# Pinning the scaling of a scan's rows in ScalarE's program order, two slots ahead of the step

## The chip, the cores and the metric

The kernel runs on one core of a Trainium2 chip. The metric is the device time of one execution in microseconds; the time of a kernel is the median of several runs. Engines are named as in the profile: PE is TensorE (PEld its weight loads), ACT is ScalarE, DVE is VectorE, POOL is GpSimd, SP issues DMAs.

## The reference

For `x` of 32 sequences of 256 tokens with 256 channels, the result is `x + ffn(cond(x))`. The first block, `cond`, is a gated state-space layer; the second has two layers of local attention and a gated feed-forward. What matters here is the scan in `cond`:

```python
xr, gate = jnp.split(x @ W_in.T, 2, axis=-1)
xr = xr + t_emb[:, None, :]
...
xn = (xc - mu) / jnp.sqrt(var + 1e-05) * ln_g + ln_b
Bm, Cm, dt = jnp.split(xn @ W_xproj.T, 3, axis=-1)
...
def step(h, inputs):
    ad, bd, xt, ct = inputs
    h = jnp.clip(h * ad[:, :, None] + bd[:, :, None] * xt[:, None, :], -10.0, 10.0)
    yt = jnp.einsum('bd,bdh->bh', ct, h)
    return (h, yt)
```

Every token is one step; the state of a sequence is 16 x 512 numbers. The second block has, for each sequence and layer, projections to q, k and v, softmax over a window of 128, and `a * gelu(g)` between two projections.

## The kernel before

**The scan.** The 32 sequences are worked in four groups of eight. With 16 states and 8 sequences the state `h` of a group fills 128 partitions x 512. A group has 256 steps, cut into 8 chunks of 32 tokens. The decay is divided out beforehand (a running product `pd`), so that a step (`step`, L665) is one VectorE instruction: add the scaled row to `h` and clip it to limits that belong to the token. Its input is a row: `xn` of token t, repeated over the 16 states and multiplied by `beta`, one number for each partition.

Each row goes through three places in the program. `load_rows` (L637), on SP's queue, loads 256 KB from `xnd` in device memory, repeated over the partitions, into a buffer `xrep` of which there are seven. `scale_row` (L658), on ScalarE, multiplies it in place by `beta`. `step` reads it on VectorE and so frees the buffer for a later load. In the first group, whose scan has no other work beside it (`alone`), half of the rows are repeated by TensorE instead (`spread_rows`, tile `bx` in PSUM) and scaled from there into an `xrep` buffer. Every fourth step, four `h` tiles are read by TensorE into `y` (`read_out`, L677).

**Slots.** The work of a group is entered into agendas by slot: slot t of a group is the place of its step t, and everything else has an offset from that. A group has two agendas: within a slot all of the first part comes ahead of the second. Loads stand at t-6 and scalings at t-1, both in the second part. The first part also holds, on ScalarE, the tanh of the convolution (`conv_th`), the copy of the raw sums, the normalising (`norm_apply`, `xn`), the squares (`norm_out`, `sq_x`), the gates and the output copy. `beta` of a chunk is ready by five slots ahead of its first step (`decays`, L606).

**The interleaving.** Attention and feed-forward of a sequence and layer are cut into stages (eight for a sequence, several sequences in flight). After each stage about two slots of the next group's scan are written into the program, so the scan of groups 1 to 3 runs beside attention and feed-forward of the groups before; the last group's have no scan beside them. All PSUM tiles of both parts share one pool of eight banks: softmax (`pT`, L1127), copies (`qT`, `kT`, `v_sb`) and gelu (`ag`, L1255) on ScalarE, and the product `ag` (L1263) on VectorE must read a bank before TensorE can have it again.

**The order on an engine.** The order written down is not the order executed. A scheduler walks the program with modelled durations and gives each engine the earliest written instruction that it believes ready[...]. An instruction whose inputs the model has as landed can therefore stand ahead of ones written before it. `tc.keep_in_program_order(ins)` ties `ins` to the instruction written before it on the same engine: it may not be issued ahead of that one. It is an ordering for the scheduler and adds no semaphore. The kernel uses it in a few places on GpSimd.

Of the kernel before, what the change touches and what calls it, by code (L numbers as in the profile page):

```python
# [73 lines left out]
def kernel(  # L74
# [29 lines left out]
    nc = tc.nc  # L104
# [111 lines left out]
    for i in range(2):  # L216
        t = const.tile([P, NI * (P + GB)], FP, tag=f"ly{i}", name=f"ly{i}")
# [3 lines left out]
    def program(ctx, exact):  # L221
# [163 lines left out]
        def group_scan(g):  # L385
# [8 lines left out]
            alone = g == 0  # L394
# [5 lines left out]
            def at(s, what, *args):  # L400
                agendas[-1].setdefault(s, []).append(partial(what, *args))
# [229 lines left out]
            def by_tensor(t):  # L631
                return alone and t % NQ < XR
# [21 lines left out]
            def scale_row(c, t):  # L654
                if by_tensor(t):
                    ck[c]["rep", t] = xp.tile([P, DI], FP, tag="xrep", name="xrep")
                bx = ck[c]["rep", t]
                nc.scalar.activation(  # L658
                    bx, ck[c].pop(("bx", t), bx), AF.Copy, scale=ck[c]["beta"][:, t : t + 1]
                )  # L660

            def step(c, t):
                bx = ck[c].pop(("rep", t))
                h_new = hp.tile([P, DI], FP, tag="h", name="h")
                nc.vector._custom_dve(  # L665
                    TENSOR_ADD_SAT, out=h_new, in0=state["h"], in1=bx,
                    s0=ck[c]["lim"][:, 0, t : t + 1], s1=ck[c]["lim"][:, 1, t : t + 1],
                )
                ck[c]["h", t] = state["h"] = h_new
# [131 lines left out]
            for c in range(NCH):  # L801
                s0 = c * CH
# [35 lines left out]
            for c in range(NCH):  # L838
                s0 = c * CH
                at(s0 - 43, load_x, c)  # L840
                for ch in range(NC_):
                    at(s0 - 40 + 2 * ch, project, c, ch)
                for ch, s in enumerate((13, 16, 17, 18)):
                    at(s0 + s, project, c, NC_ + ch)
                at(s0 - 27, raw_sums, c)
                for j in range(NJ):
                    at(s0 - 26 + 4 * j, norm_turn, c, j)
                at(s0 - 8, figures_out, c)
                for t in range(CH):
                    if not by_tensor(t):  # L850
                        at(s0 + t - 6, load_rows, c, t)
                    if by_tensor(t) and t % XR == 0:
                        at(s0 + t - 4, spread_rows, c, t)
                    at(s0 + t - 1, scale_row, c, t)
                for hb in range(CH // TB):
                    s = s0 + hb * TB
                    at(s - 9 if alone else s + 7, load_skip, c, hb)
                    at(s + 23, out_turn, c)
                for d in range(KM):
                    at(s0 + 43 + 2 * d, project_y, c, d)  # L860
# [3 lines left out]
        def scan_slots(groups):  # L864


            slots, scans = {}, [group_scan(g) for g in groups]
            for part in range(2):
                for i, agendas in enumerate(scans):
                    for s, what in agendas[part].items():  # L870
                        slots.setdefault(i * S + s, []).extend(what)
            for s in range(min(slots), max(slots) + 1):
                for what in slots.get(s, ()):
                    what()
                yield s
# [525 lines left out]
        s0 = done[0]  # L1401
# [130 lines left out]
```

## Time and profile before

| | us |
|---|---|
| median of 3 runs | 3999.52 (3998.8 to 4003.98) |
| profiled execution | 3989.48 |
| its span, first to last instruction | 3987.7 |
| first and last scaling (L658) | 50.7 to 3104.3 |
| ScalarE busy | 2321.3 |
| VectorE busy | 2638.7 |
| loads of a row (L637) | 896, of 256 KB |

The span is what the profile's views refer to. A group's line gives the instruction's line, engine and tiles, then its total and mean duration, and then the idle time of its engine just before it with what ended it. A wait line says who waited for whom, with the total in us, how often, and the longest. What an idle engine costs depends on whether another engine waits for it.

### The profile page before, as it was taken

The page shows a single profiled execution, that of the slowest core. Times are in us where ns is not written, and L with a number is a line of the kernel's source. Part 1 is how long each engine was busy: PE and PEld are TensorE (multiplying, and loading weights), DVE is VectorE, ACT ScalarE, POOL GpSimd, SP SyncE. Part 2 cuts the span into 40 slices and gives each one's busy share as a digit, 9 for nine tenths or more (in the row PEclk, how much of TensorE's full clock was granted, in tenths as well). Part 3 has the DMA queues.
Part 4 walks back from the last instruction along what each step waited for, and adds up shares of the span by engine and source line. Part 5 has one row for each costly group of instructions (what it writes and reads, how often), then busy time and mean ns, then how long its engine had stood idle before and what let it go on. Part 6 is the DMA issues. An engine that isn't in the chain of part 4 may idle for free.

```text
span 3987.7 us, 57891 instructions
## 1 busy us (share of the span) xinstructions
PE 3769.4 (95%) x20540; PEld 2359.2 (59%) x20540; DVE 2638.7 (66%) x5241; ACT 2321.3 (58%) x3893; POOL 1739.2 (44%) x1784
## 2 busy tenths in 40 slices
PE   7899889999999999999999999999999999999999
PEld 3333345666656666666666666566666666666666
DVE  6888887777766766767676677676677544444443
ACT  3555556666666566566666656556666555555553
POOL 4443364444444444544445444344444343433431
PEclk8999899999999999999999999999999999999999
DMA  5444533333433434233343434323333111000000
GB/s 152 116 119 118 159 111 110 89 107 103 106 98 97 124 109 128 84 93 94 91 112 94 118 106 116 101 83 101 94 101 103 36 36 44 1 17 20 18 14 23
DMA packets 360414, 353.51 MB, mean 89 GB/s; under 512 B 173795, under 2 KB 220212, under 8 KB 359988
## 3 DMA queue, kind: packets, MB, share of 16 engines
q1 hardware_dynamic: 275666, 337.71, 29.4%
q10 hardware_dynamic: 84450, 12.01, 1.9%
q8 instruction: 165, 2.70, 0.3%
q14 instruction: 133, 1.09, 0.1%
HBM read 314.49 MB, written 33.55 MB: 87 GB/s over the span
## 4 chain that ended last, share of the span: by engine, by line
PE 44%; DVE 16%; ACT 13%; DMA 11%; POOL 9%; issue 5%; ACTq 1%; SPq 0%; DVEq 0%; POOLq 0%
DMA xrep<-xnd 10%; PE ps_qkv L912 9%; PE pa L1247 8%; PE po_f L1275 5%; DVE h L665 5%; PE y L677 3%; ACT xrep L658 3%; PE ps_wo L962 3%; PE sc L1118 3%; PE ov L1156 2%; POOL rn L944 2%; ACT L1255 2%; DVE acc L454 2%; PE ps_in L407 2%; ACT L1127 2%
## 5 line engine op out<-in xcount | busy, mean ns | idle before, releaser
L658 ACT ACTIVATE xrep<-xrep,beta 128x512 f32<-128x512 f32 x896 | 631.1, 722 | 692.2 <-DMA xrep<-xnd 532.4
L665 DVE CUSTOM_DVE_ANT_0 h<-h,xrep,lim 128x512 f32<-128x512 f32 x1024 | 918.6, 897 | 52.7 <-PE y L677 12.5
L912 PE MATMUL ps_qkv<-qkv,res 128*128 128x512 f32 x1536 | 718.0, 604 | 34.6 <-ACT qT L956 21.7
L1247 PE MATMUL pa<-hT,w 128*128 128x256 f32 (+1 forms) x3072 | 693.0, 388 | 28.0 <-ACT pT L1127 26.8
L936 POOL TENSOR_TENSOR rot<-rot,swp 128x512 f32<-128x512 f32 x256 | 344.1, 1344 | 766.3 <-DVE swp L933 621.5
L1247 PEld LDWEIGHTS pa<-hT,w 128*128 128x128 f32 (+1 forms) x3072 | 502.4, 179 | 192.1 <-issue 63.3
L1263 DVE SCALAR_TENSOR_TENSOR ag<-pa,b_sb,ag 128x256 f32<-128x256 f32 (+1 forms) x448 | 213.1, 476 | 594.6 <-ACT ag L1255 593.2
L912 PEld LDWEIGHTS ps_qkv<-qkv,res 128*128 128x128 f32 x1536 | 279.2, 192 | 314.6 <-issue 247.4
L944 POOL TENSOR_TENSOR rn<-ss,neg_half 128x8 f32<-128x8 f32 x256 | 444.2, 1735 | 11.5 <-DVE ss L942 1.6
L1275 PE MATMUL po_f<-ag,w 128*128 128x256 f32 (+1 forms) x1536 | 385.4, 392 | 17.9 <-DVE res L1286 9.3
L677 PE MATMUL y<-h,ly 128*32 128x512 f32 x2048 | 369.1, 620 | 20.1 <-DVE h L665 19.5
L1275 PEld LDWEIGHTS po_f<-ag,w 128*128 128x128 f32 (+1 forms) x1536 | 273.9, 189 | 124.3 <-issue 44.4
L407 PE MATMUL ps_in<-xg,w_in_sb 128*128 128x256 f32 x1024 | 285.9, 410 | 18.0 <-DMA xg<-in_xT_dram 10.4
L945 POOL TENSOR_TENSOR rot<-rot,rn 128x512 f32<-128x512 f32 x256 | 287.7, 1124 | 20.0
L1206 POOL TENSOR_TENSOR rstd<-ve,neg_half 128x1 f32<-128x1 f32 x128 | 77.0, 602 | 486.6 <-DVE ve L1204 486.6
L407 PEld LDWEIGHTS ps_in<-xg,w_in_sb 128*128 128x128 f32 x1024 | 190.8, 199 | 145.7 <-issue 62.0
L928 DVE TENSOR_TENSOR rot<-ps_qkv,rc_sb 128x512 f32<-128x512 f32 x256 | 175.6, 686 | 139.0 <-ACT sq L925 137.8
L1127 ACT ACTIVATE pT<-sc 128x512 f32<-128x512 f32 x384 | 208.3, 594 | 94.9 <-PE sc L1118 93.3
L454 DVE SCALAR_TENSOR_TENSOR acc<-xr,wc_sb,acc 128x256 f32<-128x256 f32 x384 | 203.4, 532 | 89.2 <-POOL acc L443 88.1
L1127 ACT ACT_TABLE_LOAD x185 | 237.4, 1283 | 24.5 <-PE sc L1118 21.5
L1255 ACT ACTIVATE ag<-pa,b_sb 128x256 f32<-128x256 f32 x320 | 151.7, 474 | 156.8 <-PE pa L1247 152.4
L1255 ACT ACT_TABLE_LOAD x186 | 238.6, 1283 | 3.3
(149 smaller groups left out, 5765.7 us busy)
## 6 DMA issues: line engine op xcount, KB each, us to landing
xrep<-xnd SPq DMA_DIRECT2D x896, 256.0 KB
xnd<-xn SPq DMA_DIRECT2D x64, 256.0 KB
qkv<-in_wqkv_dram SPq DMA_DIRECT2D x24, 512.0 KB
xd<-xnd SPq DMA_DIRECT2D x192, 64.0 KB
w<-in_w_dram SPq DMA_DIRECT2D x80, 128.0 KB
xg<-in_xT_dram SPq DMA_DIRECT2D x64, 128.0 KB
ys<-yo ACTq DMA_DIRECT2D x64, 128.0 KB
res<-ys SPq DMA_DIRECT2D x32, 256.0 KB
```

Of the source, the lines that this page charges most:

```text
L407: nc.tensor.matmul(ps, w_in_sb[:, k, ch * P : (ch + 1) * P], ck[c]["xg"][:, k], start=(k == 0), stop=(k == KM - 1),)
L658: nc.scalar.activation(bx, ck[c].pop(("bx", t), bx), AF.Copy, scale=ck[c]["beta"][:, t : t + 1])
L665: nc.vector._custom_dve(TENSOR_ADD_SAT, out=h_new, in0=state["h"], in1=bx, s0=ck[c]["lim"][:, 0, t : t + 1], s1=ck[c]["lim"][:, 1, t : t + 1],
L677: nc.tensor.matmul(ck[c]["y", hb][32 * q : 32 * q + 32, :], ly[hb % 2][:, 32 * t : 32 * t + 32], ck[c].pop(("h", hb * TB + t)), start=(i = ...
L912: nc.tensor.matmul(ps, res[b][:, k, t0 : t0 + W], wt["qkv", a][:, k], start=(k == 0), stop=(k == KM - 1),)
L936: nc.gpsimd.tensor_add(rot, rot, swp)
L944: nc.gpsimd.tensor_tensor(rn, ss, neg_half, ALU.pow)
L945: nc.gpsimd.tensor_mul(rot, rot, bc(rn, 2, DH))
L1127: nc.scalar.activation(p, banks[r], AF.Exp)
L1247: nc.tensor.matmul(pg if x else pa, wt["w1", m][:, k, x], self.h[:, k], start=(k == 0), stop=(k == KM - 1),)
L1255: nc.scalar.activation(ag[0:n], pg, AF.Gelu, bias=b1g)
L1275: nc.tensor.matmul(self.po[:, d], wt["w2", 0][r0 : r0 + n, m, d * P : (d + 1) * P], self.ag[m][r0 : r0 + n], start=(m == 0), stop=(m == le ...
```

## The change

Two edits in `group_scan`. `scale_row` is tied to its place in ScalarE's program order, in all groups but the first. And the scaling is entered two slots ahead of its step, rather than one, in all groups.

```diff
@@ -655,9 +655,12 @@
                 if by_tensor(t):
                     ck[c]["rep", t] = xp.tile([P, DI], FP, tag="xrep", name="xrep")
                 bx = ck[c]["rep", t]
-                nc.scalar.activation(
+                scaled = nc.scalar.activation(
                     bx, ck[c].pop(("bx", t), bx), AF.Copy, scale=ck[c]["beta"][:, t : t + 1]
                 )
+                if not alone:
+
+                    tc.keep_in_program_order(scaled)
 
             def step(c, t):
                 bx = ck[c].pop(("rep", t))
@@ -851,7 +854,7 @@
                         at(s0 + t - 6, load_rows, c, t)
                     if by_tensor(t) and t % XR == 0:
                         at(s0 + t - 4, spread_rows, c, t)
-                    at(s0 + t - 1, scale_row, c, t)
+                    at(s0 + t - 2, scale_row, c, t)
                 for hb in range(CH // TB):
                     s = s0 + hb * TB
                     at(s - 9 if alone else s + 7, load_skip, c, hb)
```

## The prediction

> **What bounds the kernel now.** I read the page from its top: busy shares, the slices over time, then the costliest groups.
>
> ```profile
> PE 3769.4 (95%) x20540; PEld 2359.2 (59%) x20540; DVE 2638.7 (66%) x5241; ACT 2321.3 (58%) x3893; POOL 1739.2 (44%) x1784
> ...
> PE   7899889999999999999999999999999999999999
> ...
> L658 ACT ACTIVATE xrep<-xrep,beta 128x512 f32<-128x512 f32 x896 | 631.1, 722 | 692.2 <-DMA xrep<-xnd 532.4
> ```
>
> TensorE is busy 95% of the span and nowhere else is an engine near that. But ScalarE (ACT), busy 58%, stands idle another 692 us in front of one line, L658, the scaling of the scan's rows, and 532 us of that ends when a row's DMA lands. The question is what this idle time does to TensorE. The windows view, cut where TensorE's share changes, gives three regimes (columns: length, then busy us and instruction count of PE, PEld, DVE, ACT, POOL):
>
> ```profile
> 0.00:460.00 460.00, 394.47 (x1478) 161.73 (x1478) 388.53 (x732) 246.97 (x455) 188.86 (x280) 0.93 0.45 125
> 460.00:3116.00 2656.00, 2512.61 (x14103) 1602.43 (x14103) 1882.58 (x3704) 1647.34 (x2774) 1227.06 (x1226) 0.99 0.37 104
> 3116.00:3987.70 871.70, 862.36 (x4962) 595.06 (x4960) 367.61 (x807) 427.03 (x664) 323.29 (x278) 1.00 0.08 22
> ```
>
> First the first group's scan alone, then scan and attention/feed-forward side by side, then a tail without scan. The tail has TensorE at 862.36/871.70 = 98.9%; the mixed stretch at 2512.61/2656 = 94.6%, so 143.4 us idle. That stretch holds 768 scan steps, 3.46 us for each slot. The waits of the mixed stretch, ScalarE's, then VectorE's (DVE), then TensorE's (total us, times, longest):
>
> ```profile
> ACT xrep L658 <- DMA xrep<-xnd: 447.0, 280, 7.7
> ACT xrep L658 <- DVE beta L606: 112.1, 20, 6.6
> ...
> DVE ag L1263 <- ACT ag L1255: 374.1, 134, 7.6
> ...
> PE pa L1247 <- ACT pT L1127: 26.8, 15, 1.9
> PE ps_qkv L912 <- ACT qT L956: 21.7, 14, 2.2
> PE ov L1156 <- DVE ag L1263: 13.6, 12, 2.1
> ```
>
> ScalarE loses 559 us before the scaling (447.0 on the row, 112.1 on `beta`); VectorE loses 374 us for the gelu that ScalarE makes; TensorE waits mostly for PSUM banks that pT, qT (ScalarE) or the product ag (VectorE) must first empty. The timeline of ScalarE shows the link (start, length, idle before):
>
> ```profile
> 1509.85 0.79 ACT L1226 ACTIVATE hT<-tp_hn,flb_sb,flg_sb 128x128 f32<-128x128 f32 x2
> 1516.02 0.72 ACT L658 ACTIVATE xrep<-xrep,beta 128x512 f32<-128x512 f32 x1 [5.38 <-DMA xrep<-xnd]
> 1516.76 1.28 ACT L1127 ACT_TABLE_LOAD   x1
> 1518.06 1.08 ACT L1127 ACTIVATE pT<-sc 128x512 f32<-128x512 f32 x2
> ...
> 1524.80 0.48 DVE L1263 SCALAR_TENSOR_TENSOR ag<-pa,b_sb,ag 128x256 f32<-128x256 f32 x1 [7.18 <-ACT ag L1255]
> ```
>
> ScalarE sits 5.38 us on a row, softmax and gelu queue behind it, and VectorE (last line, from its own timeline) sits 7.18 us for that gelu. After this VectorE makes three steps in a row, four buffers come free together and four loads go out together at 1526.07: the next wait for a row is prepared by this one.
>
> [...] nothing passed the waiting scaling for 5.38 us. [...] a bunch of loads issued from 1512.39 is first used at 1516.02, 3.63 us later. [...] So I checked whether "busy" hides waiting: the ps_qkv matmul (L912) takes 603 ns in 800 to 2800 us and 597 ns in the tail, pa (L1247) 392 against 384. One to two per cent, with a granted clock of 0.99 against 1.00, so the visible idle time is nearly all there is to win.
>
> **The change part by part.** Nothing is computed anew, no semaphore is added, and the scaling stays 722 ns. Its two parts:
>
> *The pin* (768 scalings, groups 1 to 3). Each is placed behind the ScalarE instruction that precedes it in the program: a same-slot one of the scan (tanh, normalising, gate copy), else one of attention or feed-forward. Today it floats forward: in the trace of before no step waits for its scaling to speak of (DVE h from ACT xrep 1.5 us in the mixed stretch), while the scaling waits 280 times for its row; it sits close behind the issue of its load. With the pin it follows two slots before its step. The load is issued at slot t-6, so four slots lie between, 4 x 3.46 = 13.8 us, against 3.63 us for a landing and 7.7 us for the longest wait. The 447 us should mostly go; the 112 us for `beta`, which is made at slot -5 of a chunk, too.
>
> *One slot earlier* (all groups). In the first group, without the pin, an xrep buffer of a row spread by TensorE is held one slot longer (at most six of seven buffers are then in use) and its PSUM bank one slot shorter. ScalarE is busy 247 of 460 us there and VectorE, at 388.5, is what that stretch hangs on. I take 0, between -5 and +5 us: 85.4 us of row waits are there, but covered by VectorE's work.
>
> *What queues behind it.* The scaling issues no DMA; SP's and POOL's queues are passed by nothing. Indirectly, SP's loads wait for steps (1651.5 us in 772 waits in the whole span, its normal state), so a late step means a late load. Behind a scaling that waits stand pT, ag, qT and hT as today.
>
> *What ends a stall next.* If ScalarE no longer waits for rows, the next late things on it are those that wait for VectorE in the mixed stretch: xn 84.5, sq_x 58.5, ad 44.4, th 33.1 us. These stay, and scalings now stand behind them.
>
> *The sum.* ScalarE's 559 us are not on the path; what counts is TensorE's 143.4 us idle. Upper end: the tail's density, 2512.61/0.989 = 2540 us, a gain of 116. How strongly rows and TensorE go together is seen in two neighbouring stretches. In 860 to 1060 us ScalarE waits 19.5 us for rows, in the next 200 us it waits 55.4:
>
> ```profile
> 860.00:1060.00 200.00, 195.84 (x1104) 127.00 (x1106) 145.76 (x293) 134.13 (x223) 93.75 (x93) 1.00 0.38 108
> 1060.00:1260.00 200.00, 183.46 (x1047) 117.28 (x1040) 135.03 (x268) 120.49 (x203) 88.15 (x88) 0.97 0.37 100
> ```
>
> 12.4 us of TensorE for 35.9 us of waiting, 0.35. Applied to 447 us this gives 154, more than all the idle time; two windows are a weak slope, and the ten other such windows from 660 us on (25.5 to 43.7 us of waiting, TensorE 94 to 96%) show less. I take half of the ceiling, 57 us: TensorE at 2512.6/2599 = 96.7%, since the VectorE waits above remain and scanning now hangs on ScalarE's order. Lower bound of the unknown: a loss, priced under C.
>
> The profiled execution took 3989.48 us (span 3987.7); minus 57 is 3932. The median of the runs is 3999.52, 10 us more; against it I forecast 3999.5 - 57 = 3942 us.
>
> **The rivals.**
>
> *A, likeliest, 0.60:* row waits go, TensorE fills to some 96 to 98.5%, gain 20 to 116 us, at 3942.
>
> *B, 0.16:* a new wait takes the place of most of the old one. For it: seven xrep buffers are still a ring from step t-7 to load t; when steps come in bunches the loads do too, and a pinned scaling whose row is late blocks ScalarE as before. Also xn, sq_x and th now stand in front of it. Against it: 13.8 us of room. If a fifth of the ceiling is kept, the gain is 23 and with a little paid elsewhere 8 to 20: about 3985.
>
> *The pin does little, 0.07:* it ties only to the one instruction before it, which may itself float forward; then the order hardly changes and the time lies within 8 us (0.2%, about what a measurement of this kernel can tell from no change): 3999.
>
> *C, slower, 0.17:* VectorE becomes the one that waits, for scalings. Today's scaling precedes its step by much; with the change by two slots, 6.9 us, and the scheduler may place the step on VectorE right behind it, so that nothing of this remains. Place: each of the 24 chunks has two xn and two sq_x on ScalarE, which wait 84.5/22 = 3.8 and 58.5/17 = 3.4 us when they do; 4 x 3.6 = 14.4 us a chunk. A step that waits on a scaling behind them holds up on VectorE everything that empties PSUM banks. If a quarter gets through to TensorE, 3.6 us x 24 = 86 us, less the 57 gained is +29: about 4029. It decides from 2.4 us a chunk on (57/24). Against it: VectorE has 374 us of waiting for ag that shrinks in exchange.
>
> **How the numbers follow.** Faster A + B = 0.76, same 0.07, slower 0.17. The range leaves out the last of A (over 115 us of gain, 0.05) and most of C: 3885 to 4012. A's own range is 3884 to 3980.
>
> **What would show it.** Right: in the mixed stretch the wait of xrep for its DMA falls from 447 to under 120 us and that for `beta` to under 20; ag's on VectorE from 374 to under 250; TensorE over 96%; the tail and the first 460 us unchanged. A new wait of DVE h for ACT xrep, now 1.5 us, of over 150 us would be C. The forecast is wrong in its main step if the row waits go and TensorE's share stays at 94.6%, or if row waits stay above 300 us.

## The result, and the profile after

The changed kernel takes 3864.13 us (median of 4 runs) against 4001.75 for the kernel before on the same chip: ratio 0.9658, interval 0.9646 to 0.967, so 3.4% faster. The forecast was 3942 us, in a range from 3885 to 4012: the measured time lies below that range, and the gain of 137.6 us is 2.4 times the 57 us forecast. The profiled execution of after took 3863.54 us (span 3861.7), 125.9 less than that of before; the rest of the 137.6 is that the profiled execution of before was 12 us quicker than its median.

First the page of after: busy shares, the engines of the chain that ended last, and the two groups of the scan. Line numbers behind L658 have moved by three (the step is L668).

```profile
PE 3744.8 (97%) x20540; PEld 2352.5 (61%) x20540; DVE 2656.7 (69%) x5241; ACT 2320.5 (60%) x3893; POOL 1727.6 (45%) x1784
...
PE 64%; DVE 16%; POOL 10%; issue 4%; DMA 3%; ACT 3%; SPq 0%; ACTq 0%; POOLq 0%; DVEq 0%
...
L668 DVE CUSTOM_DVE_ANT_0 h<-h,xrep,lim 128x512 f32<-128x512 f32 x1024 | 931.0, 909 | 174.0 <-ACT xrep L658 143.9
...
L658 ACT ACTIVATE xrep<-xrep,beta 128x512 f32<-128x512 f32 x896 | 621.7, 717 | 92.2 <-DMA xrep<-xnd 81.7
```

The scaling costs what it cost (717 ns, 722 before), but ScalarE's idle time in front of it is 92 us, not 692. In the chain that ended last, TensorE has 64% where it had 44%, and DMA 3% where it had 11%; this is the line of before:

```profile
PE 44%; DVE 16%; ACT 13%; DMA 11%; POOL 9%; issue 5%; ACTq 1%; SPq 0%; DVEq 0%; POOLq 0%
```

The idle time before the step is new.

The three regimes, cut at the last step as before (length, then busy us and count of PE, PEld, DVE, ACT, POOL; clock, DMA share, GB/s):

```profile
0.00:460.00 460.00, 394.63 (x1480) 162.50 (x1480) 387.11 (x731) 244.32 (x451) 189.59 (x280) 0.92 0.47 125
460.00:2997.00 2537.00, 2494.67 (x14186) 1598.90 (x14184) 1905.96 (x3713) 1650.81 (x2781) 1215.20 (x1227) 1.00 0.40 109
2997.00:3861.70 864.70, 855.51 (x4880) 591.06 (x4876) 363.62 (x799) 425.36 (x661) 322.81 (x277) 1.00 0.08 22
```

The first 460 us are as they were. The mixed stretch is 119 us shorter (2537 for 2656), the tail 7. In the mixed stretch TensorE's idle time fell from 143.4 to 42.3 us (98.3% busy), and its busy time from 2512.6 to 2494.7, although 83 more matmuls lie in the stretch.

Waits of that stretch, ScalarE for rows, then VectorE, then TensorE:

```profile
ACT xrep L658 <- DMA xrep<-xnd: 1.7, 4, 0.7
...
DVE h L668 <- ACT xrep L658: 143.9, 63, 4.5
DVE ag L1266 <- ACT ag L1258: 82.1, 65, 5.8
...
PE ov L1159 <- DVE ag L1266: 7.6, 14, 0.6
```

Row waits went from 447 us to 1.7. VectorE waits 82 us for gelu instead of 374, and 144 instead of 1.5 for scalings. Of the waits of TensorE's matmuls only one is left above 7 us in total. In this piece of ScalarE's timeline of after, both idle stretches end with TensorE (over the whole mixed stretch its longest wait is one for VectorE, 167 us for the `th` of the convolution):

```profile
1520.94 1.28 ACT L1130 ACT_TABLE_LOAD   x1
1523.37 1.08 ACT L1130 ACTIVATE pT<-sc 128x512 f32<-128x512 f32 x2 [1.14 <-PE sc L1121]
1524.47 1.28 ACT L1258 ACT_TABLE_LOAD   x1
1528.28 0.47 ACT L1258 ACTIVATE ag<-pa,b_sb 128x256 f32<-128x256 f32 x1 [2.53 <-PE pa L1250]
```

### The profile page after: what moved, and what is told of

It is laid out like the page before. It is cut to its first block, busy times and chain, and to the rows that moved or that the text cites. A ratio compares the mean times of both kernels' runs of the same rounds, so it can differ in the third digit from the quotient of the medians.

```text
span 3861.7 us, 57676 instructions
## 1 busy us (share of the span) xinstructions
PE 3744.8 (97%) x20540; PEld 2352.5 (61%) x20540; DVE 2656.7 (69%) x5241; ACT 2320.5 (60%) x3893; POOL 1727.6 (45%) x1784
## 4 chain that ended last, share of the span: by engine, by line
PE 64%; DVE 16%; POOL 10%; issue 4%; DMA 3%; ACT 3%; SPq 0%; ACTq 0%; POOLq 0%; DVEq 0%
PE ps_qkv L915 13%; PE pa L1250 12%; PE po_f L1278 8%; DVE h L668 6%; PE y L680 4%; PE sc L1121 4%; PE ps_wo L965 3%; PE ps_in L407 3%; PE ov L1159 3%; DVE acc L454 3%; POOL rn L947 3%; PE rb L1174 2%; PE tr_qk L954 2%; DMA xrep<-xnd 2%; PE sc L1114 2%
## 5 line engine op out<-in xcount | busy, mean ns | idle before, releaser
L668 DVE CUSTOM_DVE_ANT_0 h<-h,xrep,lim 128x512 f32<-128x512 f32 x1024 | 931.0, 909 | 174.0 <-ACT xrep L658 143.9
L1250 PE MATMUL pa<-hT,w 128*128 128x256 f32 (+1 forms) x3072 | 683.3, 384 | 1.3 <-ACT xn L533 1.1
L658 ACT ACTIVATE xrep<-xrep,beta 128x512 f32<-128x512 f32 x896 | 621.7, 717 | 92.2 <-DMA xrep<-xnd 81.7
L939 POOL TENSOR_TENSOR rot<-rot,swp 128x512 f32<-128x512 f32 x256 | 331.4, 1294 | 708.7 <-DVE swp L936 433.6
L680 PE MATMUL y<-h,ly 128*32 128x512 f32 x2048 | 371.1, 617 | 19.6 <-DVE h L668 17.8
L454 DVE SCALAR_TENSOR_TENSOR acc<-xr,wc_sb,acc 128x256 f32<-128x256 f32 x384 | 191.7, 502 | 80.9 <-POOL acc L443 78.4
```

The source lines that it names most:

```text
L454: nc.vector.scalar_tensor_tensor(acc, xr[:, :, k : k + CH], wc_sb[:, ch, k : k + 1], acc, ALU.mult, ALU.add,)
L658: scaled = nc.scalar.activation(bx, ck[c].pop(("bx", t), bx), AF.Copy, scale=ck[c]["beta"][:, t : t + 1])
L668: nc.vector._custom_dve(TENSOR_ADD_SAT, out=h_new, in0=state["h"], in1=bx, s0=ck[c]["lim"][:, 0, t : t + 1], s1=ck[c]["lim"][:, 1, t : t + 1],
L680: nc.tensor.matmul(ck[c]["y", hb][32 * q : 32 * q + 32, :], ly[hb % 2][:, 32 * t : 32 * t + 32], ck[c].pop(("h", hb * TB + t)), start=(i = ...
L939: nc.gpsimd.tensor_add(rot, rot, swp)
L1250: nc.tensor.matmul(pg if x else pa, wt["w1", m][:, k, x], self.h[:, k], start=(k == 0), stop=(k == KM - 1),)
```

## The experiments

The theory: a floating scaling stands right behind its load's issue; ScalarE waits for the landing, and gelu and softmax behind it come late, so that TensorE runs out of PSUM banks. (In the timeline of before, the scores `sc` of a softmax were done at 1512.49 us, and `pT` was made from them only at 1518.06, behind the scaling that stood for its row until 1516.02.) The rivals: the earlier slot brings the gain; or any new order does and the gain has nothing to do with rows.

The experiments ran on chips on which before took 3979 to 3994 us, so times are compared by their ratio to before. "The stretch" below is the time from the 274th step (the end of the first group and its drain) to the last, taken from the starts of the steps in each trace: 2635 us before, 2513 after. It leaves out the first group, which some experiments slow down.

**The pin alone.**

```diff
-                    at(s0 + t - 2, scale_row, c, t)
+                    at(s0 + t - 1, scale_row, c, t)
```

> The pin alone: scalings are tied as in the changed kernel, but stay one slot ahead of the step. Theory 1 (ScalarE's waits for rows leave TensorE idle [...]; the pin takes the waits away): 3855 to 3890 us, row waits in the mixed stretch under 100 us as with the change. If one slot (3.3 us) is too little lead, VectorE's wait for scalings grows from 144 to over 250 us while TensorE is hardly touched. Theory 2 (the earlier slot brings the gain): 3960 to 4010 us. Theory 3 (any new order by the scheduler does as well, the gain is luck): a time anywhere between 3860 and 4010 that does not follow the row waits.

3870.22 us, ratio 0.9721 (0.9705 to 0.9737); row waits 4.4 us; the stretch 2525. The pin does nearly all of it. VectorE's wait for scalings was 150 us, not over 250: one slot less hardly changed it.

**The slot alone.**

```diff
-                    at(s0 + t - 1, scale_row, c, t)
+                    at(s0 + t - 2, scale_row, c, t)
```
(on the kernel before, without the pin)

> The slot alone: scalings are entered two slots ahead of the step and float as before. Theory 1: 3985 to 4015 us, row waits in the mixed stretch stay at 400 to 500 us, since a floating scaling is placed by readiness and not by its slot. Theory 2: 3860 to 3900 us. Theory 3: anything between, without relation to the row waits.

3978.3 us, ratio 0.9997 (0.9987 to 1.0007): nothing. In its trace 763 of the 768 floating scalings stand at the same place in ScalarE's order as before, and its waits in the mixed stretch are close to those of before:

```profile
ACT xrep L658 <- DMA xrep<-xnd: 408.4, 267, 6.8
DVE ag L1263 <- ACT ag L1255: 365.4, 132, 7.3
```

So the second theory falls: a floating scaling hardly takes notice of its slot.

**No row to wait for, floating and pinned.** In groups 1 to 3 nothing is loaded, and the scaling reads a constant tile:

```diff
-                if by_tensor(t):
+                if by_tensor(t) or not alone:
                     ck[c]["rep", t] = xp.tile([P, DI], FP, tag="xrep", name="xrep")
                 bx = ck[c]["rep", t]
+                if not alone:
+                    ck[c]["bx", t] = lng_sb
...
-                    if not by_tensor(t):
+                    if not by_tensor(t) and alone:
                         at(s0 + t - 6, load_rows, c, t)
```

> Order as before (no pin, one slot), but in groups 1 to 3 no row is loaded: the scaling takes a constant tile that lies in SBUF (the gain of the first norm) instead of the token's row; the scan of these groups then works on other data, all else is kept. Theory 1 (the wait for rows is the cause): without a row to wait for the floating order is harmless: 3850 to 3890 us, though the waits for beta (112 us) may stay. Theory 3 (the floating order itself is bad, whatever the row): 3940 to 4000 us.

3854.4 us, ratio 0.9671 (0.9655 to 0.9687), the stretch 2505: nearly the order of before, without rows, is as fast as the changed kernel. (96% of ScalarE's other instructions keep their order; the scalings stand a median of two instructions earlier.) So a floating order is not slow by itself. Its waits from 479 to 2984 us:

```profile
ACT xrep L660 <- DVE h L667: 297.8, 291, 6.3
DVE ag L1265 <- ACT ag L1257: 140.5, 84, 4.8
DVE h L667 <- PE y L679: 127.2, 63, 3.4
ACT xrep L660 <- DVE beta L606: 108.6, 20, 6.6
...
PE pa L1249 <- ACT pT L1129: 18.3, 14, 1.4
```

This surprised me: ScalarE still stands idle for 406 us in front of the scaling, for a free buffer or for `beta`, and little is lost. Idle time of ScalarE there is not in itself the cost. The kernel also moves less data (31 GB/s in place of 103 in that stretch), which this run alone does not separate from the wait; the next one helps.

> The same constant tile in place of the loaded rows of groups 1 to 3, with the pin and two slots. Theory 1: the row waits are gone in the changed kernel already, so taking away the rows adds nothing but quieter DMA queues: 3840 to 3870 us, within 20 us of the floating kernel without rows. Theory 3: 60 us or more below the floating one.

3847.57 us, ratio 0.9664 (0.9648 to 0.968), the stretch 2498, 7 us below the floating one. Pin or not makes little odds once there is no row to wait for. This run also bounds the effect of moving less data: under the pin, where row waits are 2 us anyway, leaving out the loads shortens the stretch by only 15 us (2513 to 2498), against 130 in the floating order.

The traces also show where TensorE pays for a wait of ScalarE. Its two largest waits before were 26.8 us for `pT` and 21.7 us for `qT`. Of the 15 waits for `pT`, 14 (26.6 us) come behind a wait of ScalarE of 6.5 or 6.6 us, and that one is for `beta`, not for a row. Of the 14 for `qT`, 13 come behind a row wait of 3.2 to 4.2 us. One of each, ScalarE's line first:

```profile
1485.45 0.72 ACT L658 ACTIVATE xrep<-xrep,beta 128x512 f32<-128x512 f32 x1 [6.62 <-DVE beta L606]
1488.44 1.78 PE L1247 MATMUL pa<-hT,w 128*128 128x256 f32 x7 [1.93 <-ACT pT L1127]
...
1440.88 0.72 ACT L658 ACTIVATE xrep<-xrep,beta 128x512 f32<-128x512 f32 x1 [3.47 <-DMA xrep<-xnd]
1443.19 1.13 PE L912 MATMUL ps_qkv<-qkv,res 128*128 128x512 f32 x2 [1.64 <-ACT qT L956]
```

The pin takes away both kinds. The floating kernel without rows keeps the waits for `beta`, and all its 18.3 us of waits for `pT` stand behind them; without rows and pinned there are none. What the waits for `beta` cost on their own no run separates; those two kernels lie 7 us apart.

**Row waits brought back under the pin.** Fewer `xrep` buffers mean that a load goes out later:

```diff
-        xp = ctx.enter_context(tc.tile_pool(name="xp", bufs=7, reuse_waits="tile"))
+        xp = ctx.enter_context(tc.tile_pool(name="xp", bufs=4, reuse_waits="tile"))
...
-                        at(s0 + t - 6, load_rows, c, t)
+                        at(s0 + t - 3, load_rows, c, t)
```

> Pinned at two slots, but with four row buffers rather than seven, loads three slots ahead: a load goes out after the step four rows back. In the changed kernel a scaling starts 16.8 us (median) after its load is issued; three slots of 3.3 us less leave 7 us against 3.6 us for a landing. Theory 1: row waits of 20 to 120 us in the mixed stretch and 3865 to 3900 us. Theory 3 (the pinned order is what counts): within 10 us of the changed kernel, whatever the row waits.

3907.19 us, ratio 0.9803 (0.9787 to 0.982). Much of that is the first group, which has fewer buffers too (its 274th step starts 39 us later than before). The stretch is 2530, with 197 us of row waits.

> Pinned at two slots, with three row buffers, loads two slots ahead: by the same sum 3.7 us are left for a landing of 3.6 us. Theory 1: the row waits come back under the pinned order, 150 to 500 us in the mixed stretch, [...]: 3910 to 4010 us. Theory 3: within 20 us of the changed kernel.

(Three buffers, loads at t-2.) 4027.68 us, ratio 1.0103 (1.0079 to 1.0127), slower than before; here the first group loses 119 us, and the stretch is 2566. From 600 to 3166 us:

```profile
ACT xrep L658 <- DMA xrep<-xnd: 422.4, 233, 7.4
DVE h L668 <- ACT xrep L658: 259.8, 164, 4.5
DVE ag L1266 <- ACT ag L1258: 88.7, 68, 7.5
```

Nearly as many row waits as before (422 for 447 us), and yet only 53 us of the 122 are given back. VectorE waits little for gelu now, and much for scalings.

**Is it the distance between scaling and step, or the floating?** Two runs on this question: before with three buffers (floating, but close to its step), and the pin with scaling and load in one slot.

```diff
-        xp = ctx.enter_context(tc.tile_pool(name="xp", bufs=7, reuse_waits="tile"))
+        xp = ctx.enter_context(tc.tile_pool(name="xp", bufs=3, reuse_waits="tile"))
...
-                        at(s0 + t - 6, load_rows, c, t)
+                        at(s0 + t - 2, load_rows, c, t)
```

> The order of before (no pin, one slot), but three row buffers and loads two slots ahead, so a floating scaling can't stand far ahead of its step. The pinned kernel with three buffers took 2566 us from step 274 to the last with 422 us of row waits, before takes 2635 with 444. If the floating order itself costs the 69 us between them: 2620 to 2680 us here, at 400 to 600 us of row waits. If it is the distance between scaling and step (a row waited for long before it is needed, gelu and softmax behind it): 2550 to 2590 us, and VectorE's waits for gelu well under the 374 us of before. The whole time is 60 to 110 us above that, since the first group too has three buffers.

4156.21 us, ratio 1.0407 (1.0383 to 1.0431), the stretch 2685, a little above the first case. From the end of a scaling to its step it is a median of 4.5 us here, 17.8 before, 3.6 in the changed kernel and 1.3 with three buffers under the pin. From 580 to 3265 us:

```profile
ACT xrep L658 <- DMA xrep<-xnd: 620.5, 334, 7.7
DVE ag L1263 <- ACT ag L1255: 309.6, 102, 7.2
DVE h L665 <- ACT xrep L658: 123.7, 103, 4.8
```

> Pinned, but in groups 1 to 3 the scaling stands in the same slot as its load (five slots ahead of the step, six row buffers, first group at two): it should start some 3.7 us after its load's issue, as in the kernel before, and far ahead of its step. Row waits in the stretch from step 274 to the last: 300 to 480 us. Theory 1a (a row wait costs TensorE most where the scaling stands far ahead of the need, since gelu and softmax wait behind a row that nobody needs yet): the stretch is near the 2635 us of before, 2590 to 2650, and VectorE waits for gelu over 200 us. Theory 1b (row waits cost the same wherever they stand under a pin, as with three buffers: 2566 us at 422 us of waits; the rest of the loss is the floating order's own): 2545 to 2580 us.

(Six buffers, load and scaling both at t-5 in groups 1 to 3.) 3864.16 us, ratio 0.9694 (0.9678 to 0.971). A miss: row waits came to only 41 us, as the pinned scaling, behind the ScalarE work written before it, started a median of 9.8 us after its load's issue, not 3.7. It does not tell the two theories apart. The stretch is all the same 2531 us, 21 more than that of the changed kernel on this chip: TensorE waits 26.0 us for `pT` in it, 14 times, each time behind a wait of ScalarE of 6.4 to 6.6 us for VectorE, this time for the input of `th`.

> Pinned, four buffers, loads and scalings in the same slot, three ahead of the step in groups 1 to 3: one slot earlier than the four-buffer kernel with two slots (197 us of row waits, 2530 us). One slot less lies between load and scaling, so 250 to 450 us of row waits. If the distance between scaling and step sets the cost of a wait, the stretch is longer than the 2566 us of three buffers at two slots; if under a pin only the amount counts, it lies on the line 2513 + 0.125 x waits, 2545 to 2570 us.

(Four buffers, load and scaling both at t-3.) 3907.26 us, ratio 0.9774 (0.9755 to 0.9793), the stretch 2516 at 161 us of row waits. Fewer waits than I expected, for the same reason, and nearly free.

Side by side, the stretch against row waits (counted in views that begin up to 21 us ahead of it):

| kernel | order | row waits, us | VectorE waits for gelu, us | stretch, us |
|---|---|---|---|---|
| no rows | floating | 0 | 141 | 2505 |
| slot alone | floating | 408 | 365 | 2627 |
| before | floating | 447 | 374 | 2635 |
| three buffers | floating | 621 | 310 | 2685 |
| no rows | pinned | 0 | 81 | 2498 |
| changed kernel | pinned | 2 | 82 | 2513 |
| four buffers, t-3 | pinned | 161 | 94 | 2516 |
| four buffers, t-2 | pinned | 197 | 82 | 2530 |
| three buffers, t-2 | pinned | 422 | 89 | 2566 |

Floating, each microsecond of row wait costs 0.29 to 0.30 ((2627 - 2505)/408, (2635 - 2505)/447, (2685 - 2505)/621). Pinned, from the changed kernel, it costs 0.02 to 0.13. That the three floating figures agree so well is in part luck: pinned kernels with under 45 us of row waits have stretches from 2477 to 2531 us, so some 25 us can come from the order alone, which is 0.06 per microsecond at 422 or 447 us of waits. The gap between 0.13 and 0.29 is wider than that on both sides together. The third theory is right to that extent: an order is worth some 25 us, but not the 122 between before and after. The distance is not it, as it is 17.8 us before and 4.5 with three floating buffers at the same price; the floating order makes a row wait dear. In the floating kernels with rows VectorE waits 310 to 374 us for gelu, in the pinned ones of the table under 100 whatever the row waits: it fits that a floating scaling gets in front of gelu while a pinned one comes behind the work written before it. That this is why, no run shows.

**Other places for the pinned scaling**, to see whether VectorE's new wait costs anything. First the changed kernel again, as a yardstick on this chip.

> The changed kernel as it is, beside the other runs of this call. Both theories: 3858 to 3870 us; it is the yardstick for the other three.

3860.22 us, ratio 0.9692 (0.9676 to 0.9708), the stretch 2510.

```diff
-                    at(s0 + t - 2, scale_row, c, t)
+                    at(s0 + t - (2 if alone else 4), scale_row, c, t)
```
(with 3 or 5 in place of 4 in the other two)

> Pinned, and in groups 1 to 3 three slots ahead of the step (first group at two). Theory 1: row waits still small, since three slots (10 us) stay between the load and the scaling against 3.6 us for a landing: 3855 to 3875 us, and VectorE's wait for scalings falls from 144 us to under 80, which brings TensorE little. Theory 3: a scatter of more than 20 us around the changed kernel.

3851.91 us, ratio 0.9673 (0.9657 to 0.9689): its interval overlaps the yardstick's, so no difference is shown. VectorE's wait for scalings stayed at 141 us; I had expected it under 80.

> Pinned, groups 1 to 3 four slots ahead of the step, seven buffers. Some 10 us (16.8 less two slots of 3.3) lie between issue and scaling, so row waits stay under 60 us: 3845 to 3870 us. If VectorE's wait for scalings (144 us with the change) cost TensorE anything, this is 5 to 15 us below the changed kernel; if not, within 5 us.

3828.62 us, ratio 0.9615 (0.9599 to 0.9631), 31.6 us below the changed kernel beside it, twice the most that I expected. This version beats both kernels. From 479 to 2955.5 us, its length and busy times, and then its waits:

```profile
479.00:2955.50 2476.50, 2455.45 (x14052) 1587.17 (x14056) 1881.35 (x3681) 1633.67 (x2751) 1205.87 (x1218) 1.00 0.38 110
```

```profile
DVE h L668 <- PE y L680: 161.6, 77, 3.4
DVE ag L1266 <- ACT ag L1258: 67.2, 51, 2.6
...
DVE h L668 <- ACT xrep L658: 16.5, 44, 3.3
...
ACT xrep L658 <- DMA xrep<-xnd: 9.4, 7, 2.7
```

TensorE stands idle for 21 us there, and VectorE now waits for TensorE (y, to free an `h`) and not for scalings.

> Pinned, seven buffers, five slots ahead in groups 1 to 3. With four slots the stretch took 2477 us and row waits were 9 us; a slot more leaves some 11 us (median) between issue and scaling, so row waits of 10 to 60 us: 3825 to 3850 us in all. Over 3845 if four slots is the optimum because row waits begin again; under 3829 if the lead over the step still pays.

3868.68 us, ratio 0.9681 (0.9663 to 0.97), the stretch 2511: as slow as two slots, but not because row waits begin again, as the expectation had it. They were 15 us, and VectorE's wait for scalings 21. With both small the gain of four slots is gone, so that gain can't be put down to VectorE's wait alone. The trace shows where the loss against four slots lies. ScalarE waits for the input of `th`, and 14 of these waits, of 5.7 to 6.6 us, stand shortly ahead of a softmax that TensorE then waits for:

```profile
ACT th L462 <- DVE acc L454: 200.2, 63, 8.1
PE pa L1250 <- ACT pT L1130: 24.6, 14, 2.2
```

With four slots ScalarE waits 181 us for `th` too, but TensorE never waits for `pT`, and its idle time in the stretch is 21 us, not 51. It is the pattern that the waits for `beta` make in before. Why four slots keep clear of it, and why four are better than three, stays open.

**The first group pinned too.**

```diff
-                if not alone:
-
-                    tc.keep_in_program_order(scaled)
+                tc.keep_in_program_order(scaled)
```

> As the changed kernel, with the first group's scalings pinned too. In the first 460 us VectorE is busy 84% and TensorE 86%; ScalarE waits 85 us for rows there. If those waits cost something, 3840 to 3860 us; if VectorE's chain of steps sets that stretch, no gain, and a step that now waits for a scaling behind other ScalarE work makes it longer: 3864 to 3900 us. I lean to the second, 3870.

3858.66 us, ratio 0.969 (0.9674 to 0.9707), the yardstick's. Row waits of the whole span fell to 4 us, but the 274th step started at 479 us, as in the yardstick (482): the first group's row waits cost nothing.

> All groups pinned, three slots ahead: the two variations that came out fast, together. If their gains are real and independent, 3840 to 3852 us, 10 to 20 us below the changed kernel on this chip; if three slots are neutral and a pinned first group too, within 8 us of it.

3850.94 us, ratio 0.9668 (0.9652 to 0.9684): the same as three slots alone.

## Why the prediction was right or wrong, point by point

- *The cause* held in the main. Row waits were forecast to fall below 120 us and fell to 1.7, gelu waits below 250 and fell to 82, TensorE above 96% and came to 98.3%. The pin alone and the slot alone show that the pin does it; the kernels without rows show that waiting for rows is most of what the pin takes away. The reading was too narrow in one place: it traced TensorE's waits to rows, but those for `pT`, the largest group, stood behind `beta` (26.6 of 26.8 us), a wait that was forecast to go and did.
- *The step that failed* is a term of the sum: "I take half of the ceiling, 57 us". The runs show no such halving: TensorE's idle time in the mixed stretch fell by 101 us of 143, and the stretch as a whole by 119. I had held back half for VectorE's waits and for scanning that "now hangs on ScalarE's order"; VectorE does wait 144 us for scalings now, but TensorE hardly lacks work for it (the largest of its waits for VectorE is 7.6 us in total).
- I had a better number and set it aside, though it was good by luck. Two neighbouring windows gave 0.35 of TensorE per microsecond of row waits, and as this overshot all the idle time I dropped it. Three floating kernels put it at 0.29 to 0.30, which is 130 us for 447. A straight line through all twelve windows gives 0.23, an estimate of 102 us, but it hangs on the two: the other ten alone show no fall.
- *The ceiling* of 116 us was too low as well, since it took TensorE's busy time as fixed. In the profiles this fell by 24.6 us (3769.4 to 3744.8): 18 in the mixed stretch, and 7 in the tail, which holds 82 matmuls fewer. I had seen the signs (603 against 597 ns, 392 against 384) and waved them off as "one to two per cent"; one per cent of 2512 us is 25 us. Most of it is the clock: the mean granted clock rose from 0.983 to 0.988. In the clock records of the two traces TensorE is busy for 108 us at half clock before and for 71 after. At half clock `ps_qkv` takes 1061 ns and `pa` 634, otherwise 592 and 379 (medians, before). So 15 to 16 of the 24.6 us are the clock's, by an estimate from these figures; the rest stays open.
- *Where the clock was at half.* In the mixed stretch the clock records show a granted clock of 0.50 in 13 pieces before, 64.9 us in all, and in 5 after, 20.5 us; each lasts 3.4, 6.8 or 10.2 us. In the 3.4 us ahead of each of the 13 pieces TensorE was busy for 3 to 43%, and ahead of seven of them the longest gap was 1.9 to 2.2 us. The waits for `pT`, of 1.9 us, are among these gaps: from 2421.9 to 2425.3 us, with one of them, TensorE is busy for 1.20 us at full clock, and from 2425.5 to 2428.7 the granted clock is 0.50. (The profile models the ends of matmuls, so the shares are rough.) Whether such a gap always lowers the clock was not shown.
- *A reading of a wait.* Of the 5.38 us that ScalarE sat on a row in the timeline, 1.75 lie ahead of that row's issue at 1512.39, which waited for a buffer; over all row waits of groups 1 to 3 it is 37 of 453 us. The 3.63 us from that issue to the first use contain the transfer of a 256 KB row, in a bunch of four.
- *The first 460 us* at 0: right (394.5 and 394.6 us of TensorE, the same length), and pinning it too changes nothing.
- *Rival B* (a ring of seven buffers that bunches) did not come; with three or four buffers it does. *The pin does little*: refuted. *Rival C* (VectorE waits for scalings): the wait came at 144 us, just under the 150 that was to mark it, but it did not cost what was priced.

## What to carry to other kernels

Look for an instruction that stands on its engine ahead of its need and waits for a transfer: what a microsecond of such a wait cost here depended on the order (0.29 to 0.30 us floating, 0.02 to 0.13 pinned), and holding the instruction at its written place gave 3.4% with no work removed. Estimate the gain from many windows of the same trace that differ in that wait, not from two, before cutting it down by feel, and allow for a busy time of TensorE that shrinks too (by 24.6 us here). After such a change, try neighbouring positions: two slots further were worth another 0.8% here, and three were not.

## What the runs showed of the hardware that I had not expected

Idle time of one size had very different prices: 406 us of ScalarE in front of the scaling cost next to nothing in the floating kernel without rows (its stretch is 7 us longer than the pinned one's), 447 us of row waits cost some 130 in before, and 422 us cost 53 under the pin. Nor did the price follow what the engine waited for: waits of some 6.6 us for `beta` (before) and for the input of `th` (five slots) each cost TensorE up to 1.9 or 2.2 us, as a softmax stood shortly behind them.
